# Attention and quantised network on one core: a longer lag for the network, a carried overshoot, GpSimd in the weights' quantisation, products of v in even pairs, an interleaved tail

## The chip, the cores and the metric

The kernel runs on one core of a Trainium2 chip. The core has five engines that work beside each other, each through its own instruction queue in order: TensorE (PE, matrix products), VectorE (DVE), ScalarE (ACT), GpSimd (POOL) and SyncE (SP), which here issues every DMA. The metric is the device time of one execution in microseconds; lower is better.

## The reference, cut to what matters

```python
xn = layernorm(x)                      # x: 8 x 1024 x 512, fp32
q, k, v = split(xn @ W_attn + b_attn)  # 16 heads of 32
att = softmax(causal(q @ k.T / sqrt(32)))
a = (att @ v) @ W_proj + b_proj
xq = fp4_quant_dequant(xn)             # blocks of 16 along the row
h = silu(xq @ wq_gate.T) * (xq @ wq_up.T)      # 1408 wide
f = fp4_quant_dequant(h) @ wq_down.T   # wq_*: weights quantised alike
out = x + a + f
```

Quantising a block takes its largest magnitude over 6 as a scale, divides, rounds to the values 0, 0.5, 1, 1.5, 2, 3, 4, 6 and multiplies by the scale again. Weights are quantised in the kernel too, 34 pieces of at most 128 x 512.

## The kernel before

The tokens are 64 tiles of 128 (8 batches of 8). Attention goes by 64 units: a unit is one pair of heads over one batch of 1024 tokens. All intermediate results between the stages lie in device memory: q and k in two halves each (high and low), v, the unnormalised y, the sums and their inverses, the transposed quantised tokens (xq_kept) and the network's result with the residual (part_kept).

Everything is written as Python generators, the streams. A stream issues some instructions and yields an estimated cost. `merge` always advances the stream that has used the smallest share of its total, so the order of the instructions on TensorE, ScalarE and SyncE is the order in which these generators were advanced. VectorE and GpSimd are ordered by the framework's scheduler. `Later(us, action)` puts an action (nearly always a DMA) off until so much estimated cost has passed.

The streams, with their lines:

- `begin` / `prepare` (L266): transposes a normalised tile (L215), keeps its quantised form, calls `load_tokens` for the tile after next and `normed` (L252, for later tiles with `quantised`, result xs) for the next tile. For each second tile it runs `project` (L307): q, k, v for 256 tokens (matmuls L315, L352), six chunks, weights from `ring_a`, two buffers of 512 KB.
- `quantised` (L182): ten VectorE instructions for a tile: L195 the block maximum, L196 to L198 small ones, L201 to L208 six of the full width.
- `weights_quantised` (L218): for each of the 34 pieces load, `quantised`, and one piece later the transposes on TensorE (L215) and ScalarE's copy (L216) into wgT, wuT or wdT.
- `prepare_late` (L282): the first eight tiles' tokens for the network, put off from the opening.
- `maxima` (L395): the row maxima of a unit's scores: matmuls L407, VectorE's mask L415 and reduce L417; at its end shT (L435).
- `weigh` (L438): scores again, with the maximum subtracted by a matmul (L466, L469), ScalarE's exponential (L477), GpSimd's causal zeroing of the diagonal block (L480), and the products with v (L449), which `weighted` issues for one or two key blocks j at a time. Two heads use different columns of the array, 33 columns each.
- `network` (L527): gate and up products (L557), `hidden`, the down products (L542); L539 adds the bias to the residual on GpSimd, L549 adds acc, and the sum part is stored. The jobs are issued in pairs.
- `finish` (L613): loads y and the inverses, multiplies (L625), multiplies by W_proj (L632, weights from `ring_p`, two loads of 512 KB a tile through one buffer), loads part and adds (L637), stores the output.

The opening interleaves `begin` of tiles 0 to 7 with EARLY = 11 pieces of weights, then does `begin` of tiles 8 and 9 beside the first unit's maxima. The main loop then runs over n = 0 to 63 and merges: `begin(n + 10)` while there are tiles (total 21.5 for odd n, 1.0 for even n), `finish` of tile n - 9 from n = 9 on, `weigh` of unit n, `maxima` of unit n + 1, and either, for n below LAG = 5, a fifth of the remaining weight pieces and of the late tiles, or, from n = 5 on, one tile's worth of the network through `up_to(net, TILE)`. After the loop five rounds run the rest of the network with the finishes, then the rest.

The lines that pick the groups of v's products:

```python
if j % 2 == 1 and waiting:
    yield weighted()
    waiting = []
waiting += fresh
```

Of the kernel before, what the change touches and what calls it, by code (L numbers as in the profile page):

```python
# [19 lines left out]
P = 128  # L20
# [7 lines left out]
def kernel(  # L28
# [44 lines left out]
    AHEAD = 10  # L73
    LAG = 5
    SCALE = HD**-0.5
# [11 lines left out]
    p8 = ctx.enter_context(tc.tile_pool(name="p8", bufs=8))  # L87
    dram = ctx.enter_context(tc.tile_pool(name="dram", bufs=3, space=DRAM))
    ps_g = ctx.enter_context(tc.tile_pool(name="ps_g", bufs=6, space=PSUM))
# [56 lines left out]
    class Ring:  # L146


        def __init__(self, pool, name, src):
            self.pool, self.name, self.src = pool, name, src  # L150
            self.cols = itertools.cycle(range(0, src.shape[2], 2 * P))
            self.loaded = []

        def load(self):
            col = next(self.cols)
# [6 lines left out]

    ring_a = Ring(p2, "wa", wa_in)
    ring_p = Ring(p1, "wp", wp_in)
# [16 lines left out]

    def quantised(src, w, xs):  # L182
# [18 lines left out]
        nc.vector.tensor_tensor(blocks(xs), blocks(src), spread(inv), ALU.mult)  # L201
        nc.vector.tensor_scalar(
            step.bitcast(I32), xs.bitcast(I32), 0x7F800000, None, ALU.bitwise_and
        )
        nc.vector.tensor_scalar(step, step, 1.0, 1.5 * 2.0**22, ALU.max, ALU.mult)
        nc.vector.tensor_tensor(xs, xs, step, ALU.add)
        nc.vector.tensor_tensor(xs, xs, step, ALU.subtract)
        nc.vector.tensor_tensor(blocks(xs), blocks(xs), spread(scale), ALU.mult)  # L208
        return xs
# [8 lines left out]
    def weights_quantised():  # L218
# [14 lines left out]
        for k, piece in enumerate(pieces):  # L233
            if k + 2 < len(pieces):
                loaded.append(load(*pieces[k + 2]))
            raw = loaded.pop(0)
            done.append((piece, quantised(raw, piece[4], raw)))
            yield 0.0
# [199 lines left out]
    def weigh(un):  # L438
        f, r0 = un.u * HU // HPC, un.u * HU % HPC
        for Q in range(2):  # L440
# [19 lines left out]
            for j in range(last + 1):  # L460
# [29 lines left out]
                yield (W - q0) * 0.00044 * 4  # L490
                if j % 2 == 1 and waiting:
                    yield weighted()
                    waiting = []
# [31 lines left out]


    def network(tiles):  # L527
        def turn(job):
# [4 lines left out]
        def down(job):  # L533
# [13 lines left out]
            if i == NI - 1:  # L547
                xr = tl.xr
                nc.vector.tensor_tensor(xr, tl.acc, xr, ALU.add)  # L549
                tl.part = dram.tile([P, D], F32, name="part_kept", bufs=NT + 6)  # L550
                Later(8.0, lambda: nc.sync.dma_start(out=tl.part, in_=xr))
            yield 0.1
# [21 lines left out]

        def load(tl):
            tl.xqT = p3.tile([P, NC, P], F32, name="xqT_in")
            nc.sync.dma_start(out=tl.xqT, in_=tl.xq)

        def jobs():
            load(tiles[0])  # L580
            for tl, following in zip(tiles, tiles[1:] + [None]):
# [7 lines left out]
        while True:  # L589
# [21 lines left out]
            older = pair  # L611

    def finish(tl):  # L613
        t = tl.t
        yT = p1.tile([P, NC, P], F32, name="yT")
        nc.sync.dma_start(out=yT, in_=tl.batch.y[:, :, t * P : (t + 1) * P].rearrange("f p t -> p f t"))
# [9 lines left out]
        yield 3.0  # L626
        po = ps_g.tile([P, D], F32, name="g")
        for half in range(2):
            cols = slice(half * 2 * P, (half + 1) * 2 * P)
            wp = ring_p.take()  # L630
            for c in range(NC):
                nc.tensor.matmul(po[:, cols], lhsT=yT[:, c, :], rhs=wp[:, c, :], start=(c == 0), stop=(c == NC - 1))  # L632
            ring_p.load()
            yield 1.7
        part = p3.tile([P, D], F32, name="res")
        nc.sync.dma_start(out=part, in_=tl.part)
        nc.vector.tensor_tensor(part, po, part, ALU.add)  # L637
        Later(6.0, lambda: nc.sync.dma_start(out=out[tl.b, t * P : (t + 1) * P, :], in_=part))
# [14 lines left out]
    class Tile:  # L653
        def __init__(self, n):
            self.n, self.b, self.t = n, n // NT, n % NT

    class Unit:
# [4 lines left out]
    def run(step):  # L662
        for cost in step:
            passed(cost)
# [12 lines left out]

    def up_to(step, total):

        spent = 0.0  # L680
        while spent < total:
            try:
                cost = next(step)
            except StopIteration:
                return
            spent += cost
            yield cost

    N = B * NT
# [11 lines left out]
    with tc.manual_schedule(  # L701
# [10 lines left out]
        PIECES = sum((w.shape[0] // P) * -(-w.shape[1] // CW) for w in (w_gate, w_up, w_down))  # L712
        EARLY = PIECES // 3
        weights_steps = weights_quantised()
        head = itertools.chain(*[begin(n) for n in range(NT)])
        merge([(head, 10.7 * NT), (up_to(weights_steps, EARLY * 0.5), EARLY * 0.5)])
        for un in units:
# [14 lines left out]
        merge([(itertools.chain(begin(NT), begin(NT + 1)), 22.0), (first_maxima(), 8.0)])  # L732
        load_biases()
        for n in range(N):
            streams = []
            if n + 2 < N:
# [11 lines left out]
            if n + AHEAD < N:  # L748
                streams.append((begin(n + AHEAD), 21.5 if n % QT == QT - 1 else 1.0))
            if n >= NT + 1:  # L750
                streams.append((finish(tiles[n - NT - 1]), 6.4))
            streams.append((weigh(units[n]), 19.0))
            if n >= LAG:
                streams.append((up_to(net, TILE), TILE))
            else:
                part = (PIECES - EARLY) / LAG * 0.5
                streams.append((up_to(weights_steps, part + 0.01), part))
                for tl in tiles[n * NT // LAG : (n + 1) * NT // LAG]:
# [52 lines left out]
```

## Time and profile before

| | us |
|---|---|
| median of three runs (lowest, highest) | 4766.83 (4761.64, 4768.15) |
| the profiled execution, its run | 4757.63 |
| its span | 4755.9 |
| mean granted TensorE clock | 0.976 of full |

The profile comes from one execution. The span is the time from the first to the last recorded instruction of that execution; the run has some 2 us around it. Sums made from the trace are to be set against the span; the median of the other runs is 11 us above it.

To read it: the page gives each engine's busy time, then the span in 40 slices of 119 us with the busy share in tenths. A group's row has line, engine, operation, output and inputs, shapes, the count, the busy time and the mean of one in ns, then the engine's idle time just before and what ended it. The record counts an fp32 product as two TensorE instructions, since it makes two passes (1408 records for 704 products at L542); the products of L407, L466 and L469, in a reduced format, have one. Matmul ends are modelled, so distances from start to start are the better measure: 429 ns for a record of 512 columns in fp32, 216 ns for 256, 231 ns for 512 in the reduced format.

Times of units, from the stamps of L498 (the copy of y, last in a unit): units 0 to 4 end 50.7 to 65.2 us apart, later even and odd units alternate around 59 and 82 us, and from unit 54 on, without `begin`, they are some 58 us apart.

### The profile page before, as it was taken

The page shows a single profiled execution, that of the slowest core. Times are in us where ns is not written, and L with a number is a line of the kernel's source. Part 1 is how long each engine was busy: PE and PEld are TensorE (multiplying, and loading weights), DVE is VectorE, ACT ScalarE, POOL GpSimd, SP SyncE. Part 2 cuts the span into 40 slices and gives each one's busy share as a digit, 9 for nine tenths or more (in the row PEclk, how much of TensorE's full clock was granted, in tenths as well). Part 3 has the DMA queues.
Part 4 walks back from the last instruction along what each step waited for, and adds up shares of the span by engine and source line. Part 5 has one row for each costly group of instructions (what it writes and reads, how often), then busy time and mean ns, then how long its engine had stood idle before and what let it go on. Part 6 is the DMA issues. An engine that isn't in the chain of part 4 may idle for free.

```text
span 4755.9 us, 54933 instructions
## 1 busy us (share of the span) xinstructions
PE 4490.6 (94%) x17876; PEld 2693.5 (57%) x17876; DVE 2794.9 (59%) x6841; ACT 1505.3 (32%) x2906; POOL 491.1 (10%) x1177
## 2 busy tenths in 40 slices
PE   7677899999999999999999999999999999999995
PEld 6445555555555555655555656556556555555553
DVE  6698466655556565656655656555656654566542
ACT  2133333333333333333333333333333333333310
POOL 0011111110110110110110011010111110111100
PEclk9888999999999999999999999999999999999997
DMA  6644434444453453544454454443454444333233
GB/s 208 181 138 137 111 102 109 132 128 130 114 150 106 123 135 107 139 132 117 125 146 118 121 146 118 123 128 115 128 145 122 132 123 127 98 98 94 65 91 108
DMA packets 582590, 590.38 MB, mean 124 GB/s; under 512 B 131616, under 2 KB 445984, under 8 KB 582304
## 3 DMA queue, kind: packets, MB, share of 16 engines
q1 hardware_dynamic: 582304, 586.88, 44.7%
q8 instruction: 142, 2.33, 0.2%
q14 instruction: 144, 1.18, 0.1%
HBM read 434.12 MB, written 152.57 MB: 123 GB/s over the span
## 4 chain that ended last, share of the span: by engine, by line
PE 83%; DVE 7%; DMA 6%; issue 1%; ACT 1%; SPq 1%; POOL 0%; DVEq 0%; ACTq 0%; POOLq 0%
PE g L557 24%; PE acc L542 11%; PE y L449 10%; PE g L315 8%; PE g L407 6%; PE g L466 5%; PE g L469 5%; PE g L632 5%; PE g L352 4%; PE g L215 2%; DMA inv_y<-inv_kept 2%; DVE scale L195 1%; DMA wp<-in_L_attn_W_proj_dram 1%; DMA qs<-qk_kept 1%; PE g L433 1%
## 5 line engine op out<-in xcount | busy, mean ns | idle before, releaser
L477 ACT ACTIVATE pr<-g 128x512 f32<-128x512 f32 (+3 forms) x1536 | 668.7, 492 | 1082.0 <-PE g L469 1072.8
L417 DVE TENSOR_REDUCE neg<-g 128x1 f32<-128x512 f32 (+3 forms) x1024 | 585.3, 582 | 230.0 <-PE g L407 225.7
L466 PE MATMUL g<-shT,pick 128*128 128x512 f32 (+3 forms) x1536 | 672.2, 447 | 20.3 <-DVE neg L417 16.3
L557 PE MATMUL g<-wgT,xqT_in 128*128 128x512 f32 (+1 forms) x1536 | 674.9, 566 | 13.8 <-DMA xqT_in<-xq_kept 13.4
L407 PE MATMUL g<-ks,qs 128*128 128x512 f32 (+3 forms) x1536 | 664.0, 477 | 18.5 <-DVE neg L417 11.4
L542 PE MATMUL acc<-wdT,hqT 128*128 128x512 f32 x1408 | 672.2, 599 | 1.4 <-ACT hqT L216 1.4
L480 POOL TENSOR_SCALAR_AFFINE_SELECT pr<-pr 128x128 f32<-128x128 f32 x1024 | 360.0, 366 | 3021.8 <-ACT pr L477 3005.5
L557 PE MATMUL g<-wuT,xqT_in 128*128 128x512 f32 (+1 forms) x1536 | 671.5, 562 | 0.0
L449 PE MATMUL y<-pr,vs 128*33 128x512 f32 (+3 forms) x3072 | 606.8, 497 | 2.9 <-POOL pr L480 2.7
L415 DVE TENSOR_TENSOR g<-g,mask 128x128 f32<-128x128 f32 x1024 | 289.3, 293 | 482.4 <-PE g L407 477.1
L469 PE MATMUL g<-qs,ks 128*128 128x512 f32 (+3 forms) x1536 | 516.9, 348 | 0.0
L315 PE MATMUL g<-xnT,wa 128*128 128x256 f32 x2048 | 486.9, 393 | 29.4 <-DVE scale L196 12.9
L315 PEld LDWEIGHTS g<-xnT,wa 128*128 128x128 f32 x2048 | 398.4, 198 | 108.2 <-ACT xnT L216 13.9
L407 PEld LDWEIGHTS g<-ks,qs 128*128 128x128 f32 x1536 | 280.4, 191 | 306.1 <-issue 139.8
L557 PEld LDWEIGHTS g<-wgT,xqT_in 128*128 128x128 f32 x1536 | 278.5, 191 | 237.5 <-issue 184.1
L557 PEld LDWEIGHTS g<-wuT,xqT_in 128*128 128x128 f32 x1536 | 276.0, 189 | 216.4 <-issue 167.8
L542 PEld LDWEIGHTS acc<-wdT,hqT 128*128 128x128 f32 x1408 | 255.7, 189 | 230.4 <-issue 215.0
L466 PEld LDWEIGHTS g<-shT,pick 128*128 128x128 f32 x1536 | 293.6, 191 | 154.4 <-issue 65.7
L469 PEld LDWEIGHTS g<-qs,ks 128*128 128x128 f32 x1536 | 293.8, 191 | 96.8 <-issue 64.6
L449 PEld LDWEIGHTS y<-pr,vs 128*33 128x33 f32 x3072 | 138.9, 110 | 354.5 <-issue 278.2
L572 DVE TENSOR_TENSOR hid<-hid,g 128x512 f32<-128x512 f32 (+1 forms) x192 | 122.7, 639 | 306.8 <-PE g L557 288.7
L632 PE MATMUL g<-wp,yT 128*128 128x256 f32 x1024 | 253.3, 392 | 47.5 <-DVE yT L625 27.9
(87 smaller groups left out, 4201.2 us busy)
## 6 DMA issues: line engine op xcount, KB each, us to landing
wa<-in_L_attn_W_attn_dram SPq DMA_DIRECT2D x194, 512.0 KB
wp<-in_L_attn_W_proj_dram SPq DMA_DIRECT2D x131, 512.0 KB
qs<-qk_kept SPq DMA_DIRECT2D x512, 128.0 KB
ks<-qk_kept SPq DMA_DIRECT2D x512, 128.0 KB
qk_kept<-high SPq DMA_DIRECT2D x128, 256.0 KB
qk_kept<-low SPq DMA_DIRECT2D x128, 256.0 KB
res<-in_L_attn_x_dram SPq DMA_DIRECT2D x72, 256.0 KB
v_kept<-v SPq DMA_DIRECT2D x64, 264.0 KB
```

Source lines behind the costliest of these rows:

```text
L315: nc.tensor.matmul(pq[:, j, :], lhsT=wa[:, c, j * P : (j + 1) * P], rhs=xnT[:, c, :], start=(c == 0), stop=(c == NC - 1),)
L407: nc.tensor.matmul(sc[:, :n], lhsT=un.qs[Q][:, r, i * P : (i + 1) * P], rhs=un.ks[h][:, r, :n], start=True, stop=True,)
L415: nc.vector.tensor_tensor(sc[:, n - P : n], sc[:, n - P : n], mask, ALU.add)
L417: nc.vector.tensor_reduce(dst, sc[:, :n], AX.X, ALU.max, negate=True)
L449: nc.tensor.matmul(y[r * 2 * HD : r * 2 * HD + VW, q0:], lhsT=un.vs[h][:, jj, r, :], rhs=pr[:, q0:], start=(j == 0), stop=(j == last), ski ...
L466: nc.tensor.matmul(w[:, q0:], lhsT=pick[:, Q * HU + r, :], rhs=un.shT[:, q0:], start=True, stop=False)
L469: nc.tensor.matmul(w[:, q0:], lhsT=un.ks[h][:, r, jj * P : (jj + 1) * P], rhs=un.qs[Q][:, r, q0:], start=False, stop=True,)
L477: nc.scalar.activation(pr[:, q0:], w[:, q0:], AF.Exp)
L480: nc.gpsimd.affine_select(out=pr[:, q0 : q0 + P], in_=pr[:, q0 : q0 + P], compare_op=ALU.is_ge, fill=0.0, base=0, pattern=[[1, P]], channe ...
L542: nc.tensor.matmul(tl.acc, lhsT=job.hqT[:, j, :], rhs=wdT[:, i, :], start=(i == 0), stop=(i == NI - 1))
L557: nc.tensor.matmul(job.g[:, : job.w], lhsT=job.tl.xqT[:, c, :], rhs=wT[:, c, job.i0 : job.i0 + job.w], start=(c == 0), stop=(c == NC - 1),)
L632: nc.tensor.matmul(po[:, cols], lhsT=yT[:, c, :], rhs=wp[:, c, :], start=(c == 0), stop=(c == NC - 1))
```

## The change

Eight edits go together:

- LAG is 8 instead of 5, and EARLY is half of the 34 pieces (17) instead of a third (11). So 17 pieces and eight late tiles are spread over eight units.
- `quantised` takes an engine for its first and last full-width product; the weights pass GpSimd.
- `weighted` is called at even j instead of odd j.
- `up_to` carries what it spent too much (or too little) into its next call.
- `begin(n + 10)` of even n has a total of 4.0 instead of 1.0.
- `finish` of tile n - 10 instead of n - 9; it loads part ahead of the products where it is there already, with its store done first if that is still put off, and makes the product in two halves with a PSUM tile and an addition each.
- From unit 55 on, W_proj stays resident in the two buffers of `ring_a`, whose loads are counted so that none comes too many.
- After the loop each of eight rounds takes one tile of the network and one finish (two in the first); the last finish begins its loads before the rest of the network.

```diff
-    LAG = 5
+    LAG = 8
...
-            done.append((piece, quantised(raw, piece[4], raw)))
+            done.append((piece, quantised(raw, piece[4], raw, nc.gpsimd)))
...
-        nc.vector.tensor_tensor(blocks(xs), blocks(src), spread(inv), ALU.mult)
+        spreader = spreader or nc.vector
+        spreader.tensor_tensor(blocks(xs), blocks(src), spread(inv), ALU.mult)
...
-        nc.vector.tensor_tensor(blocks(xs), blocks(xs), spread(scale), ALU.mult)
+        spreader.tensor_tensor(blocks(xs), blocks(xs), spread(scale), ALU.mult)
...
-                if j % 2 == 1 and waiting:
+                if j % 2 == 0 and waiting:
...
-                tl.part = dram.tile([P, D], F32, name="part_kept", bufs=NT + 6)
-                Later(8.0, lambda: nc.sync.dma_start(out=tl.part, in_=xr))
+                tl.part = dram.tile([P, D], F32, name="part_kept", bufs=NT + 8)
+                tl.stored = Later(8.0, lambda: nc.sync.dma_start(out=tl.part, in_=xr))
...
+        def load_part():
+            tl.stored.now()
+            part = p3.tile([P, D], F32, name="res")
+            nc.sync.dma_start(out=part, in_=tl.part)
+            return part
...
-        po = ps_g.tile([P, D], F32, name="g")
+        part = load_part() if tl.part is not None else None
         for half in range(2):
+            po = ps_g.tile([P, 2 * P], F32, name="g")
             cols = slice(half * 2 * P, (half + 1) * 2 * P)
-            wp = ring_p.take()
+            wp = resident[half] if resident else ring_p.take()
             for c in range(NC):
-                nc.tensor.matmul(po[:, cols], lhsT=yT[:, c, :], rhs=wp[:, c, :], start=(c == 0), stop=(c == NC - 1))
-            ring_p.load()
+                nc.tensor.matmul(po, lhsT=yT[:, c, :], rhs=wp[:, c, :], start=(c == 0), stop=(c == NC - 1))
+            if not resident:
+                ring_p.load()
+            if part is None:
+                part = load_part()
+            nc.vector.tensor_tensor(part[:, cols], po, part[:, cols], ALU.add)
             yield 1.7
-        part = p3.tile([P, D], F32, name="res")
-        nc.sync.dma_start(out=part, in_=tl.part)
-        nc.vector.tensor_tensor(part, po, part, ALU.add)
...
-    def up_to(step, total):
-
+    def up_to(step, total, over=[0.0]):
+
+        total += over[0]
         spent = 0.0
         while spent < total:
...
             spent += cost
             yield cost
+        over[0] = total - spent
...
-        EARLY = PIECES // 3
+        EARLY = PIECES // 2
...
+            if n == N - AHEAD + 1:
+                for half in range(2):
+                    wp = p2.tile([P, NC, 2 * P], F32, name="wa")
+                    nc.sync.dma_start(out=wp, in_=wp_in[:, :, half * 2 * P : (half + 1) * 2 * P])
+                    resident.append(wp)
...
-                streams.append((begin(n + AHEAD), 21.5 if n % QT == QT - 1 else 1.0))
-            if n >= NT + 1:
-                streams.append((finish(tiles[n - NT - 1]), 6.4))
+                streams.append((begin(n + AHEAD), 21.5 if n % QT == QT - 1 else 4.0))
+            if n >= LAG + 2:
+                streams.append((finish(tiles[n - LAG - 2]), 6.4))
...
+                if n == LAG - 1:
+                    Later(20.0, lambda: load(tiles[0]))
...
-        left = [finish(tiles[n]) for n in range(N - NT - 1, N)]
-        for n in range(N - LAG, N):
-            count = 1 if n in (N - LAG, N - 1) else 2
-            some, left = left[:count], left[count:]
-            merge([(up_to(net, TILE), TILE), (itertools.chain(*some), 6.4 * count)])
-        next(left[0])
+        for n in range(N, N + LAG):
+            some = [finish(tiles[m]) for m in ([n - LAG - 2] if n == N else []) + [n - LAG - 1]]
+            merge([(up_to(net, TILE), TILE), (itertools.chain(*some), 6.4 * len(some))])
+        end = finish(tiles[N - 1])
+        passed(next(end))
         run(net)
-        for step in left:
-            run(step)
+        run(end)
```

More of the change, by code (lines that the diff above doesn't have):

```diff
@@ L87 @@
     p8 = ctx.enter_context(tc.tile_pool(name="p8", bufs=8))
-    dram = ctx.enter_context(tc.tile_pool(name="dram", bufs=3, space=DRAM))
+    dram = ctx.enter_context(tc.tile_pool(name="dram", bufs=4, space=DRAM))
     ps_g = ctx.enter_context(tc.tile_pool(name="ps_g", bufs=6, space=PSUM))
@@ L146, with __init__ @@
     class Ring:
-        def __init__(self, pool, name, src):
-            self.pool, self.name, self.src = pool, name, src
+        def __init__(self, pool, name, src, count=None):
+            self.pool, self.name, self.src, self.count = pool, name, src, count
             self.cols = itertools.cycle(range(0, src.shape[2], 2 * P))
@@ L154, in load @@
         def load(self):
+            if self.count is not None:
+                self.count -= 1
+                if self.count < 0:
+                    return
             col = next(self.cols)
@@ L161, in take @@
             return self.loaded.pop(0)
-    ring_a = Ring(p2, "wa", wa_in)
+    ring_a = Ring(p2, "wa", wa_in, B * NT // QT * 3 * D // (2 * P))
     ring_p = Ring(p1, "wp", wp_in)
@@ L179, in load_biases, with quantised @@
             ring_p.load()
-    def quantised(src, w, xs):
+    def quantised(src, w, xs, spreader=None):
         nb = w // BLOCK
@@ L524, in invert, with load @@
             Later(12.0, lambda: nc.sync.dma_start(out=over(un.batch.inverses[un.u]), in_=z))
+    def load(tl):
+        tl.xqT = p3.tile([P, NC, P], F32, name="xqT_in")
+        nc.sync.dma_start(out=tl.xqT, in_=tl.xq)
     def network(tiles):
@@ L573, in hidden @@
             job.hq = quantised(job.hid, job.w, job.hid)
-        def load(tl):
-            tl.xqT = p3.tile([P, NC, P], F32, name="xqT_in")
-            nc.sync.dma_start(out=tl.xqT, in_=tl.xq)
         def jobs():
-            load(tiles[0])
             for tl, following in zip(tiles, tiles[1:] + [None]):
@@ L611, in network @@
             older = pair
+    resident = []
     def finish(tl):
         t = tl.t
+        def load_part():
[3 more added lines that the diff above has]
+            return part
         yT = p1.tile([P, NC, P], F32, name="yT")
@@ L655, in __init__ @@
             self.n, self.b, self.t = n, n // NT, n % NT
+            self.part = None
     class Unit:
@@ L676, in merge @@
                 live.remove(s)
-    def up_to(step, total):
+    def up_to(step, total, over=[0.0]):
+        total += over[0]
         spent = 0.0
         while spent < total:
-            try:
-                cost = next(step)
-            except StopIteration:
+            cost = next(step, None)
+            if cost is None:
                 return
@@ L712 @@
         PIECES = sum((w.shape[0] // P) * -(-w.shape[1] // CW) for w in (w_gate, w_up, w_down))
-        EARLY = PIECES // 3
+        EARLY = PIECES // 2
         weights_steps = weights_quantised()
         head = itertools.chain(*[begin(n) for n in range(NT)])
-        merge([(head, 10.7 * NT), (up_to(weights_steps, EARLY * 0.5), EARLY * 0.5)])
+        merge([(head, 10.7 * NT), (up_to(weights_steps, EARLY * 0.5, [0.0]), EARLY * 0.5)])
         for un in units:
@@ L733 @@
         load_biases()
+        late = [0.01]
         for n in range(N):
+            if n == N - AHEAD + 1:
[3 more added lines that the diff above has]
+                    resident.append(wp)
             streams = []
@@ L756 @@
                 part = (PIECES - EARLY) / LAG * 0.5
-                streams.append((up_to(weights_steps, part + 0.01), part))
+                streams.append((up_to(weights_steps, part, late), part))
+                if n == LAG - 1:
+                    Later(20.0, lambda: load(tiles[0]))
                 for tl in tiles[n * NT // LAG : (n + 1) * NT // LAG]:
```

## The prediction

> **What bounds the kernel now.** I read the page's engine and slice lines first, to see who is the bound and where it isn't.
>
> ```profile
> PE 4490.6 (94%) x17876; PEld 2693.5 (57%) x17876; DVE 2794.9 (59%) x6841; ACT 1505.3 (32%) x2906; POOL 491.1 (10%) x1177
> PE   7677899999999999999999999999999999999995
> PEclk9888999999999999999999999999999999999997
> ```
>
> TensorE is the bound from the fifth slice to the last but one. The first 500 us and the last 60 us are where it is not, and there its clock is lower too. So I cut the span at the stage borders, which I took from the stamps of L435 (one per attention unit) and of L498 (end of a unit): the opening, units 0 to 4 (no network in them), units 5 to 63, the tail. The windows view gives, for each: length, then busy us of PE, PEld, DVE, ACT, POOL, then clock, DMA share, GB/s.
>
> ```profile
> 13.00:144.00 131.00, 109.58 (x489) 91.38 (x488) 84.17 (x190) 28.50 (x61) 4.88 (x8) 0.93 0.71 223
> 144.00:194.00 50.00, 28.25 (x109) 21.71 (x107) 32.37 (x87) 5.61 (x12) 0.55 (x1) 0.83 0.70 194
> 194.00:489.00 295.00, 218.51 (x1000) 143.21 (x1000) 249.35 (x655) 95.81 (x206) 42.86 (x94) 0.84 0.46 128
> 489.00:4557.00 4068.00, 3990.78 (x15866) 2356.03 (x15865) 2358.85 (x5763) 1361.54 (x2605) 433.95 (x1052) 0.99 0.44 121
> 4557.00:4756.00 199.00, 143.12 (x418) 80.72 (x416) 65.32 (x133) 12.53 (x22) 4.03 (x3) 0.87 0.35 105
> ```
>
> In units 0 to 4 VectorE is busy 85% and TensorE waits for it; POOL is nearly free. The waits view, first in 194:489, then in 600:4500, and the rows of the costliest groups say what stands behind it:
>
> ```profile
> PE g L215 <- DVE hid L208: 48.4, 3, 17.4
> PE g L466 <- DVE neg L417: 13.0, 7, 4.7
> ...
> PE g L215 <- DVE xs L208: 39.6, 11, 7.8
> ...
> DVE res L637 <- DMA res<-part_kept: 218.8, 26, 23.3
> ...
> L539 POOL TENSOR_TENSOR res<-res,bp 128x512 f32<-128x512 f32 x64 | 85.0, 1328 | 597.4 <-DMA res<-in_L_attn_x_dram 467.4 <-DVE hid L207 37.6 <-DVE hid L572 33.8
> ```
>
> Three stalls of up to 17 us for a quantised weight piece early; eleven stalls later for xs, the quantised tokens of the next tile; and VectorE standing at L637 for the reload of part. The chain's last lines show the tail: each of the last finishes is serial.
>
> ```profile
> 4710.64 4.29 DMA inv_y<-inv_kept
> 4714.95 0.05 DVEq L625
> 4715.15 0.70 DVE yT L625
> 4715.89 3.79 PE g L632 x8
> 4719.70 3.83 DMA wp<-in_L_attn_W_proj_dram
> 4723.57 3.42 PE g L632 x8
> ```
>
> One finish costs 21 us there (4715.9 to 4736.8), of which 7 us are products at a falling clock; elsewhere its 16 products take 3.45 us.
>
> **What the Trainium skill says.** "TensorEngine Tiling (Array Packing)", Key Properties: changing the tiling mode drains TensorE. The trace agrees: L449 is 33 columns wide, and a group of its products takes 0.34 us (one j) or 0.37 us (two j) more than start-to-start times of the same shapes give, against 0.06 us for a stretch without one. "GPSIMD Engine Reference", 3.1: an elementwise tensor_tensor costs 1.96 times VectorE's. Here L539 has 1328 ns, VectorE's like shapes 690 ns: 1.92. "Advanced Engine Details and Errata", VectorE Performance Modes: the second SBUF port is shared and the two interfere. Ten two-input VectorE instructions that lie beside an L539 average 0.97 us, the others 0.69 us. "TensorE: Matmul & The Clock Gate", What's actually happening: half clock after an idle window of 3.4 us. The trace has 143 us at half clock before 505 us and about 40 between there and 4600.
>
> **The change, part by part**, against the profiled execution's span (4755.9 us; its run 4757.6, the median of the runs 4766.8, so I add 11 at the end).
>
> *v's products in even pairs.* Before, a unit's groups are j0, j1-2, j3 for the first half and j0, 1-2, 3-4, 5-6, 7 for the second: 8. After: 2 and 4. Two groups fewer in each of 64 units, 128 x 0.30 us (0.35 less the 0.06 background) = 38 us, all on TensorE. Bounds: 30 and 45. In every unit that is 0.6 us. The products of j are still issued one j behind their exponentials, so no new wait.
>
> *Opening (0 to 194).* EARLY goes from 11 to 17 pieces. A piece on VectorE is 4.8 us (reduce 0.68, small ones 0.70, four of 0.69, two of 0.43); with the first and last product on GpSimd 3.5 us. So 17 x 3.5 - 11 x 4.8 = +7 us of VectorE, plus its wait at L207 for GpSimd: 1.33 us and some issue, at most 17 x 1.5 = 25 us, plus slower neighbours (0.28 us each). TensorE gets 6 x 0.44 us of transposes. VectorE is 64% busy in 13:144, so most is covered by its gaps; what is not delays xt, at whose transposes TensorE already stops 3 to 5 us, four times. I take +15; bounds 0 and +45. The rstd power on GpSimd now queues behind the products; that is in it.
>
> *Units without network: 8 instead of 5.* Before 295 us, 59 a unit. VectorE per unit after: maxima and small ones 18.5 (1121 us of L415 and L417 over 64 units, plus 1), begin 8.9, one late tile 6.6, 17/8 pieces of 3.5 = 7.5: 41.5 in single durations. Before, the same sum is 5 x 27.4 + 22 x 4.8 + 8 x 6.6 = 295, of which the overlapping of neighbours leaves 249 busy, in 295 us elapsed. So what 41.5 takes is about 41.5 us, and 3 to 4 for GpSimd waits: 45. TensorE per unit: scores, maxima and v 21.3, groups 1.8, begin 11.2, transposes 1.4: 36, but 26 in even units and 46 in odd ones (project falls in those). Even: VectorE's 40; odd: TensorE's 46 at a clock of 0.92: 50. Again 45. The stage is 8 x 45.5 = 365 (bounds 304: TensorE's 36 at 0.95; 472: 59 as now). The affine_selects now share GpSimd's queue with 4.3 products of 1.33 a unit, 6 us of 45; that cover holds unless VectorE is late for GpSimd. load(tiles[0]) before unit 8 removes the 13.4 us wait of L557 for xqT_in at 489.
>
> *Units with network: 56 instead of 59.* From L498: units 13 to 52 take 71.3 us each, units 55 to 62 (no begin) 58.4. Off these: 0.6 for the groups; 0.45 for the carried overshoot (before, 59.9 network tiles lay in 59 units, 0.9 x 29.5 us; this moves work into the tail and is no gain); and in units with begin 1.4 for stalls: 50 us of TensorE gaps over 1 us between 600 and 4500, of which 40 wait for xs, and some 16 lost at half clock, over 49 units. They go because begin at 4.0 instead of 1.0 puts the next tile's normed and quantised at a quarter of an even unit, not at its end where L637 stands in the way too; part is now asked for at half a unit and before wp, not behind it. What is late next there: nothing over 1 us that I find. 46 x 68.9 + 10 x 57.4 - 7 (no finish in two units) = 3736. The same sum for before gives 4077 against 4068 measured, so I take 3727. Bounds: 3700 and 3800 (the stalls stay, 66 us).
>
> *Tail.* Before, 199 us for 4.1 tiles and 9 finishes. After: 8 tiles at 30.5 (33.3, 38.3, 37.1 us between ends of acc, less 3.45 for each finish beside them) = 244, nine finishes 31, 3 for hidden waits. wp stays in two buffers that the attention ring has left, so no 3.6 us load between halves; yT and inv of the last tile are loaded ahead. Then acc's add 0.7, store 4.5, reload 4.6 (4.1 landing at the end of before), add 0.7, store 3.0: 14. Together 292. Bounds 285 and 320.
>
> Queues: the moved part load is one DMA a finish, issued by SP ahead of two wp loads instead of behind them; the 131 wp loads fall by 38 (the last 19 finishes use the kept copies). dram's fourth buffer, part_kept's two and the Ring's count cost nothing: they allocate, or stop two loads nobody takes.
>
> Sum: 194 + 15 + 365 + 3727 + 292 = 4593, 163 below 4755.9. On the median: 4766.8 - 163 = 4604.
>
> **Rivals.** (1) *The early units stay at VectorE's pace, 59 us*, since it stands still while GpSimd works: 8 x 59 = 472, 4711. For: VectorE's order is strict, and L207 comes directly behind its GpSimd producer. Against: a wait of 1.5 us cannot eat what 1.3 us less per piece and the thinner spread (2.1 pieces a unit, not 4.6) give. (2) *They fall to TensorE's pace*: 304, 4543. For: VectorE reached 85% before. Against: odd and even units differ by 20 us of TensorE work. (3) *The change doesn't do what it says in the long stage*: pairs save little since merge cuts the stream anew and the xs stalls only move: +38 +60, 4702. For: the drain is paid at each switch, whoever follows. Against: groups are counted in the order of issue, 6 a unit. (4) *Slower*: GpSimd's in-order queue, with affine_selects and rstd in it, holds each piece, and VectorE behind it, in the opening and the early units. At 10 us instead of 1.5 a piece it is 17 x 8.5 = 145 in units and some 115 in the opening: 4864. It decides from 7 us a piece. For: POOL waits in order. Against: POOL is 15% busy in 194:489.
>
> **How the numbers follow.** Forecast 0.50, (1) 0.15, (2) 0.14, (3) 0.13, (4) 0.08. The likeliest is 4604. Its own bounds, taken as independent, give about 4555 to 4660; taking in most of (1), (2) and (3) the range is 4530 to 4712. Faster by over 0.2% (9.5 us, about what a measurement can tell here): the first four, 0.91; slower 0.08; within, 0.01.
>
> **What would show it.** 384 groups of L449 instead of 512; unit stamps 45 us apart in units 0 to 7, and 1.5 to 2 us closer in pairs later; no L215 wait for xs; GpSimd products of 1.3 to 1.5 us; PEclk near 0.9 in the early units; one finish after the last acc, some 14 us. I am wrong if GpSimd's broadcast product takes over 3 us, if early units stand above 55, or if the tail's tiles lie above 35 us.

## The result and the profile after

The changed kernel takes 4774.91 us (median of 14 runs), the kernel before 4765.12 us (14 runs beside them): ratio 1.0024, 95% interval 1.0016 to 1.0032. It is slower by some 10 us where 163 us less were forecast. The profiled execution has a span of 4773.9 us.

The page's engine and slice lines of the changed kernel:

```profile
PE 4510.9 (94%) x17876; PEld 2724.1 (57%) x17876; DVE 2764.2 (58%) x6837; ACT 1483.7 (31%) x2892; POOL 548.3 (11%) x1245
PE   7678899999999999999999999999999999999999
PEclk9789999999999999999999999999999999999999
```

The tail is now full to the end, as planned. TensorE's busy time has grown by 20 us with the same 17876 records: "busy" counts modelled ends, so the sum of the work can't be read from it. The windows view, cut at the same borders (opening in two parts, early units, units with the network, tail; columns as before):

```profile
13.00:164.00 151.00, 115.19 (x505) 96.15 (x504) 97.42 (x215) 31.03 (x67) 42.22 (x42) 0.87 0.65 202
164.00:213.00 49.00, 29.56 (x115) 22.96 (x114) 31.57 (x84) 5.51 (x12) 3.71 (x4) 0.81 0.76 203
213.00:616.00 403.00, 331.86 (x1564) 223.13 (x1565) 284.56 (x762) 143.64 (x315) 85.72 (x176) 0.92 0.52 143
616.00:4493.00 3877.00, 3762.75 (x14888) 2237.06 (x14887) 2198.82 (x5458) 1273.73 (x2449) 401.04 (x996) 0.99 0.43 117
4493.00:4774.00 281.00, 270.98 (x808) 144.19 (x806) 146.80 (x303) 28.55 (x51) 10.25 (x8) 1.00 0.19 59
```

| stage | before | forecast | after |
|---|---|---|---|
| opening | 194 | 209 | 213 |
| early units (5; 8; 8) | 295 | 365 | 403 |
| units with the network (59; 56; 56) | 4068 | 3727 | 3877 |
| tail (network tiles: 4.1; 8; 8) | 199 | 292 | 281 |

So 150 us of the miss lie in the long stage and 38 in the early units; the tail is better than forecast by 11. In the long stage a pair of units with `begin` (an even and an odd one, from the stamps of the copy of y, units 14 to 53) takes 143.8 us on average. Forecast were 2 x 68.85 = 137.7, before had 142.5. The waits view of TensorE for the long stage (700 to 4400 us), then for the early units (us in total, times, longest):

```profile
PE g L412 <- DVE neg L422: 41.1, 22, 1.9
PE g L471 <- ACT hid L578: 24.1, 22, 1.1
PE g L471 <- ACT pr L482: 16.7, 22, 1.0
...
PE y L454 <- POOL pr L485: 21.8, 16, 6.1
PE g L438 <- DVE scale L200: 14.8, 3, 5.2
PE g L220 <- POOL hid L213: 12.5, 2, 9.7
```

The stalls for xs are gone, as forecast. In their place are waits that are there 22 times, once for each pair of units in the window: 41 us in sum for a place in PSUM, where the products land, that VectorE's maxima (L422) hold, and smaller ones. Before, the same wait stood there 4 times (600 to 4500 us):

```profile
PE g L407 <- DVE neg L417: 5.5, 4, 2.5
```

The pairs are alike to a fraction of a us: the fastest takes 143.0 us, the middle one 143.6. A stall that is in one is in all.

What VectorE does then, from the timeline of one pair (start, duration, instruction; lines between left out):

```profile
1488.69 0.62 DVE L422 TENSOR_REDUCE neg<-g 128x1 f32<-128x512 f32 x1
...
1489.43 0.69 DVE L206 TENSOR_TENSOR hid<-hid,inv 128x512 f32<-128x512 f32 x1
1490.04 0.68 DVE L206 TENSOR_TENSOR xs<-xt,inv 128x512 f32<-128x512 f32 x1
...
1494.39 0.68 DVE L213 TENSOR_TENSOR hid<-hid,scale 128x512 f32<-128x512 f32 x1
1494.99 0.68 DVE L213 TENSOR_TENSOR xs<-xs,scale 128x512 f32<-128x512 f32 x1
1495.60 0.29 DVE L420 TENSOR_TENSOR g<-g,mask 128x128 f32<-128x128 f32 x1
1495.80 0.68 DVE L422 TENSOR_REDUCE neg<-g 128x1 f32<-128x512 f32 x1
```

and TensorE's side of it (the bracket is the idle time before, and what ended it):

```profile
1493.91 0.50 PE L471 MATMUL g<-shT,pick 128*128 128x512 f32 x1 [0.75 <-ACT pr L482]
1494.26 0.40 PE L474 MATMUL g<-qs,ks 128*128 128x512 f32 x1
1496.53 0.58 PE L412 MATMUL g<-ks,qs 128*128 128x256 f32 x1 [1.88 <-DVE neg L422]
```

Two quantisations, the network's hid and the next tile's xs, run interleaved from 1489 to 1495.6, and between a maximum's end and the next mask lie 6.3 us. TensorE goes on as long as it has places in PSUM, stops for 1.9 us, and goes on at half clock for 3.4 us. In 700 to 4400 us the trace's clock record has 75 us at half clock, before the change 38.

The chain's last lines show the tail: the last down products, the addition of acc, the store and the reload of part (lines between left out).

```profile
4761.26 2.86 PE acc L551 x6
...
4764.19 0.70 DVE res L558
...
4764.91 2.02 DMA part_kept<-res
...
4766.95 2.92 DMA res<-part_kept
```

### The profile page after: what moved, and what is told of

The parts are those of the page before. It is cut to its first block, busy times and chain, and to the rows that moved or that the text cites. A ratio compares the mean times of both kernels' runs of the same rounds, so it can differ in the third digit from the quotient of the medians.

```text
span 4773.9 us, 55008 instructions
## 1 busy us (share of the span) xinstructions
PE 4510.9 (94%) x17876; PEld 2724.1 (57%) x17876; DVE 2764.2 (58%) x6837; ACT 1483.7 (31%) x2892; POOL 548.3 (11%) x1245
## 4 chain that ended last, share of the span: by engine, by line
PE 79%; DVE 8%; ACT 3%; DMA 2%; issue 2%; POOL 1%; SPq 0%; ACTq 0%; DVEq 0%; POOLq 0%
PE g L566 23%; PE acc L551 12%; PE y L454 10%; PE g L320 8%; PE g L412 5%; PE g L471 5%; PE g L646 5%; PE g L474 4%; PE g L357 4%; PE g L220 2%; DVE neg L422 1%; ACT pr L482 1%; DMA qs<-qk_kept 1%; DVE scale L199 1%; DMA inv_y<-inv_kept 1%
## 5 line engine op out<-in xcount | busy, mean ns | idle before, releaser
L412 PE MATMUL g<-ks,qs 128*128 128x512 f32 (+3 forms) x1536 | 725.3, 509 | 66.4 <-DVE neg L422 44.7
L551 PE MATMUL acc<-wdT,hqT 128*128 128x512 f32 x1408 | 695.3, 617 | 1.4 <-ACT hqT L221 1.4
L485 POOL TENSOR_SCALAR_AFFINE_SELECT pr<-pr 128x128 f32<-128x128 f32 x1024 | 346.3, 350 | 2661.1 <-ACT pr L482 2649.5
L471 PE MATMUL g<-shT,pick 128*128 128x512 f32 (+3 forms) x1536 | 599.5, 398 | 55.2 <-ACT hid L578 24.1
L422 DVE TENSOR_REDUCE neg<-g 128x1 f32<-128x512 f32 (+3 forms) x1024 | 583.0, 580 | 102.4 <-PE g L412 94.8
L412 PEld LDWEIGHTS g<-ks,qs 128*128 128x128 f32 x1536 | 285.4, 193 | 327.2 <-issue 147.9
L551 PEld LDWEIGHTS acc<-wdT,hqT 128*128 128x128 f32 x1408 | 266.6, 197 | 259.2 <-issue 235.3
L454 PEld LDWEIGHTS y<-pr,vs 128*33 128x33 f32 x3072 | 159.7, 110 | 406.3 <-issue 235.9
L471 PEld LDWEIGHTS g<-shT,pick 128*128 128x128 f32 x1536 | 294.6, 192 | 163.7 <-issue 45.3
L331 ACT ACTIVATE full<-g,bqk 128x256 f32<-128x256 f32 x256 | 107.4, 471 | 625.8 <-PE g L412 265.0
L638 DVE TENSOR_TENSOR yT<-yT,inv_y 128x512 f32<-128x512 f32 x64 | 44.1, 689 | 431.6 <-DMA inv_y<-inv_kept 363.5
```

Source lines behind the costliest of these rows:

```text
L412: nc.tensor.matmul(sc[:, :n], lhsT=un.qs[Q][:, r, i * P : (i + 1) * P], rhs=un.ks[h][:, r, :n], start=True, stop=True,)
L422: nc.vector.tensor_reduce(dst, sc[:, :n], AX.X, ALU.max, negate=True)
L454: nc.tensor.matmul(y[r * 2 * HD : r * 2 * HD + VW, q0:], lhsT=un.vs[h][:, jj, r, :], rhs=pr[:, q0:], start=(j == 0), stop=(j == last), ski ...
L471: nc.tensor.matmul(w[:, q0:], lhsT=pick[:, Q * HU + r, :], rhs=un.shT[:, q0:], start=True, stop=False)
L485: nc.gpsimd.affine_select(out=pr[:, q0 : q0 + P], in_=pr[:, q0 : q0 + P], compare_op=ALU.is_ge, fill=0.0, base=0, pattern=[[1, P]], channe ...
L551: nc.tensor.matmul(tl.acc, lhsT=job.hqT[:, j, :], rhs=wdT[:, i, :], start=(i == 0), stop=(i == NI - 1))
```

## The experiments

All edits are to the changed kernel unless said otherwise. "Pair" is the mean of pairs of units 14 to 53 in the profile, "early" the time of one early unit. Three of the eight edits were not undone alone: `finish` in halves, the resident W_proj and the interleaved tail.

| run | us | ratio to before (95% interval) | pair | early |
|---|---|---|---|---|
| before | 4765 | 1 | 142.5 | 59.3 |
| changed | 4774.9 | 1.0024 (1.0016, 1.0032) | 143.8 | 50.4 |
| e1_begin_late | 4880.1 | 1.0241 (1.0228, 1.0255) | 148.3 | 50.9 |
| e2_odd_pairs | 4690.9 | 0.9845 (0.9832, 0.9859) | 139.8 | 52.1 |
| e3_lag5 | 4732.2 | 0.9935 (0.9923, 0.9948) | 141.3 | 56.7 |
| e4_dve_only | 4765.4 | 0.9998 (0.9990, 1.0006) | 144.0 | 50.0 |
| e5_no_carry | 4748.9 | 0.9968 (0.9955, 0.9980) | 143.2 | 50.5 |
| e6_pause | 4722.3 | 0.9911 (0.9899, 0.9924) | 141.6 | 50.5 |
| e7_late_own_tile | 4778.5 | 1.0025 (1.0016, 1.0034) | 144.0 | 51.2 |
| e8_odd_begin_late | 4815.6 | 1.0108 (1.0095, 1.0122) | 145.7 | 51.0 |
| e9_odd_lag5 | 4737.7 | 0.9943 (0.9930, 0.9955) | 142.2 | 56.6 |
| e10_before_begin4 | 4719.5 | 0.9910 (0.9895, 0.9925) | 140.6 | 57.8 |
| e11_odd_no_carry | 4684.2 | 0.9829 (0.9815, 0.9842) | 140.2 | 52.1 |
| e12_odd_lag5_dve | 4728.5 | 0.9926 (0.9913, 0.9938) | 142.2 | 57.4 |
| e13_begin2 | 4700.3 | 0.9862 (0.9848, 0.9875) | 139.9 | 51.2 |
| e14_odd_begin2 | 4652.4 | 0.9761 (0.9748, 0.9775) | 137.7 | 52.4 |
| e15_all_early | 4797.7 | 1.0067 (1.0053, 1.0080) | 144.0 | 46.9 |
| e16_pause_begin2_free | 4664.1 | 0.9786 (0.9772, 0.9799) | 139.7 | 51.1 |
| e17_pause_begin2 | 4673.2 | 0.9808 (0.9793, 0.9823) | 139.4 | 51.0 |
| e18_odd_begin2_dve | 4635.6 | 0.9729 (0.9714, 0.9744) | 137.5 | 51.5 |

### One edit undone at a time

The place of begin:

```diff
-                streams.append((begin(n + AHEAD), 21.5 if n % QT == QT - 1 else 4.0))
+                streams.append((begin(n + AHEAD), 21.5 if n % QT == QT - 1 else 1.0))
```

> The changed kernel with one number undone: begin of even units has the total 1.0 again instead of 4.0. Theory A (bunching): at 4.0 each even unit does its transposes, copies and the next tile's quantisation in its first quarter, beside the network's quantisation and, early, beside a late tile that needs the same xqT buffer. Then each pair of units loses some 4.5 us of TensorE in the long stage and each even unit of the first eight some 10 us. Expected 4774.9 - 23 x 4.5 - 4 x 10 = about 4630, less what xs stalls come back (at most 50): 4630 to 4680, and the first eight units at 45 us each. Theory B (the gain went elsewhere: drains, the carried overshoot, the lag): within 20 us of the changed kernel. Theory C: the xs stalls come back in full, above 4775.

It was 105 us slower than the changed kernel: theory C. The waits of TensorE in its long stage:

```profile
PE g L220 <- DVE xs L213: 133.7, 22, 6.9
PE g L471 <- ACT hid L578: 24.0, 22, 1.1
```

The stall for xs, which before had in 11 places, is there in each pair, 6 us long. So the new place is worth a lot here, and bunching at 4.0 is not the whole answer; but what this run compares with is a stall that is worse than before's.

The grouping:

```diff
-                if j % 2 == 0 and waiting:
+                if j % 2 == 1 and waiting:
```

> The changed kernel with v's products in the old grouping (8 groups a unit instead of 6). If the pairs gave what I counted, 128 more groups of 0.30 us: 38 us slower than the changed kernel, about 4813. If the wait for the last exponentials and their causal zeroing ate the gain (theory B): within 10 us of it.

84 us faster than the changed kernel, where 38 us slower or no difference was expected. The new grouping, priced with the narrowest bounds of all, costs 84 us here. I count a group from the start of the record before it to the start of the second record after it, less what records of the same shapes take from start to start elsewhere. By this count a pair of units (14 to 53) spends 6.6 us on six groups a unit and 6.5 us on eight: nothing was saved. The last group of each half is why: with six groups it takes 0.42 to 1.18 us, 0.70 on average, with eight 0.34. Nothing of its own stream lies between the scores of the last block j and the products that need its exponentials and their zeroing.

The 4.0 us by which the pairs differ lie in the order of the other streams. TensorE's waits in the long stage are, with the old grouping,

```profile
PE g L471 <- DVE neg L422: 19.0, 27, 2.2
PE g L412 <- ACT pr L482: 17.6, 26, 0.7
PE g L471 <- ACT pr L482: 16.4, 22, 0.7
```

With one more of 0.7 us these are 54 us in sum, where the changed kernel's are 108, and L412's stall for the maxima is not there. At half clock TensorE spends 7 us instead of 75. In both kernels the two quantisations run interleaved in each of the 20 even units from 14 to 53. But here the next maximum or mask comes after 4.9 us instead of 6.3, and TensorE stands for 0.7 us at L412 instead of 1.9.

The lag (with two finishes in each of five last rounds):

```diff
-    LAG = 8
+    LAG = 5
...
-            if n >= LAG + 2:
-                streams.append((finish(tiles[n - LAG - 2]), 6.4))
+            if n >= 10:
+                streams.append((finish(tiles[n - 10]), 6.4))
```

> The changed kernel with LAG 5: weights and late tiles spread over five units, network from unit 5 on, finish still of tile n - 10, two finishes in each of five last rounds. If stages without the network cost what they do in the changed kernel (50 us a unit against 36 of TensorE work), three such units fewer and three tiles more beside attention give 3 x 14 = 42 us less, minus what five units pay for more weight pieces each: 4735 to 4760. If the lag is neutral: within 10 us of the changed kernel. If the lag was a gain: above 4785.

43 us faster than the changed kernel, just below the range named. Taken alone this reads as a loss by the longer lag. The later run with the old grouping corrects it. With LAG 5 the two quantisations meet in none of the 20 even units.

GpSimd's share:

```diff
-            done.append((piece, quantised(raw, piece[4], raw, nc.gpsimd)))
+            done.append((piece, quantised(raw, piece[4], raw)))
```

> The changed kernel with the weights' quantisation on VectorE alone. By my sum GpSimd saves 17 x 1.3 = 22 us of VectorE in the first eight units and costs about 10 in the opening: 10 to 25 us slower than the changed kernel. If GpSimd's queue is what holds the early units (rival 4 in small), it is 20 us or more faster.

10 us faster without GpSimd, neither of the two. The opening takes 202 us instead of 213, the early units 400 instead of 403. The products on GpSimd were not slow (in the changed kernel 1.17 and 1.10 us for 128x512), but VectorE's time saved in the early units bought nothing, and in the opening GpSimd's share cost 11 us.

### What the lock and the wait are worth

The lock: with the carried overshoot each pair of units repeats the one before, so a stall in one is in all. The wait: that of the last groups for their exponentials.

The network's overshoot not carried (the same in the tail's rounds):

```diff
-                streams.append((up_to(net, TILE), TILE))
+                streams.append((up_to(net, TILE, [0.0]), TILE))
...
```

> The changed kernel without the carried overshoot for the network (each unit's call starts from zero; the weights keep theirs). With the carry the traces repeat from pair to pair to a tenth of a us, so a stall that falls in one pair falls in all 20. Theory P (phase lock): without it stalls come in some pairs only, and each unit with the network takes 0.45 us of it ahead: 20 to 60 us faster than the changed kernel, 4715 to 4755. Theory Q: stalls are set by what lies in a quarter unit, not by the lock: within 12 us.

26 us faster, as theory P said. Its pairs range from 138.7 to 153.3 us, where the changed kernel's lie between 143.0 and 146.0. The mean of the pairs is nearly the same (143.2). The units with the network take the same in sum, 14 us less with `begin` and 13 more without, and the tail 257 us instead of 281, since each unit took a little of the network ahead. So the pairs are locked by the carry, but nearly all that this run gains is work taken out of the tail at no cost elsewhere, not stalls, which theory P had in mind.

A pause ahead of the last groups:

```diff
+            yield 1.5
             yield weighted()
             yu = p2.tile([P, W], F32, name="yu")
...
-            streams.append((weigh(units[n]), 19.0))
+            streams.append((weigh(units[n]), 22.0))
```

> The changed kernel with an idle entry of cost 1.5 in the stream ahead of the last group of v's products of each half (and 22 instead of 19 for the stream's total), so that other streams' work lies between the last scores and the products that need their exponentials. Theory W (the last group waits for the last exponentials and their zeroing, on TensorE): the wait of some 2.1 us a pair of units in the long stage goes, groups stay at six with 0.33 us each: 50 us or more faster than the changed kernel, below 4725. Theory Q (the new grouping only moves the other streams): no clear gain, within 20 us of 4775.

53 us faster, as theory W said. By the count above the groups take 5.2 us a pair of units instead of 6.6, the last ones 0.46 us on average instead of 0.70. The weight loads' wait for GpSimd's zeroing in the long stage, first of the changed kernel, then of this one:

```profile
PEld y L454 <- POOL pr L485: 88.2, 201, 0.8
```

```profile
PEld y L454 <- POOL pr L485: 24.3, 43, 0.8
```

The pause moves the other streams too, so not all of the 53 us is this wait. The quantisations still run interleaved in all 20 even units, but L412's stall for the maxima is gone, and at half clock TensorE spends 48 us instead of 75. Shorter waits stand in its place, about as much in sum:

```profile
PE g L471 <- DVE neg L422: 24.5, 42, 1.7
PE g L412 <- ACT pr L482: 23.7, 48, 0.7
```

A late tile's tokens put back into their own tile:

```diff
-        xqT = p1.tile([P, NC, P], F32, name="xqT")
+        if own:
+            xqT = xq.rearrange("p (c e) -> p c e", e=P)
+        else:
+            xqT = p1.tile([P, NC, P], F32, name="xqT")
...
```

> The changed kernel in which a late tile's transposed tokens go back into the tile they came from, so that it doesn't share the one xqT buffer with the tile of begin. ScalarE stood 9.7 us for that buffer's store in an even early unit, and v's products waited 6 us behind it. If that is what made the first eight units 403 us instead of the 365 forecast: 20 to 35 us faster than the changed kernel, 4740 to 4755, with the early even units some 6 us shorter. If VectorE's load is what sets them: within 8 us.

No gain. ScalarE's wait for the buffer's store (44 us in the early units) is gone, but the early units take as long with other waits in its place (the lines of this kernel are three further down):

```profile
PE g L415 <- ACT full L334: 22.2, 4, 6.0
PE g L220 <- DVE res L213: 21.0, 3, 7.4
PE g L220 <- POOL hid L213: 13.7, 2, 9.8
```

Old grouping and old place of begin (the edits of the first two runs together):

> The changed kernel with both undone: old grouping of v's products and begin of even units at 1.0. At 1.0 with the new grouping the stall for xs was there in each pair of units (6 us). If that is the stall's own doing, this is about 105 us slower than with the old grouping and 4.0 (4691): 4780 to 4810. If grouping and place of begin act on each other, it lies below 4750.

4816, so 125 us slower than with the old grouping and 4.0, a little above the range named: TensorE waits 22 times for xs, 124 us in sum. With the carry that stall comes whatever the grouping.

### Two edits at once, and one alone

Old grouping and LAG 5:

> The changed kernel with the old grouping of v's products and LAG 5. If the two losses are independent: 4775 - 84 - 43 = about 4648. If LAG 5 gained only because it shifted the streams against the new grouping: 4680 to 4700.

Neither: 4738, 47 us slower than the old grouping with LAG 8. So the lag's sign depends on the grouping: 43 us lost by LAG 8 with the new one, 47 gained with the old one. The grouping's sign depends on the lag as well: at LAG 5 the new one is 6 us the faster (4732 against 4738). The pairs say why it cannot be priced alone: 141.3 (5, new), 143.8 (8, new), 142.2 (5, old), 139.8 (8, old). With LAG 5 and the old grouping a stall of 2.5 us for VectorE's shift (L438) comes in each pair.

The kernel before with begin of even units at 4.0, nothing else:

```diff
-                streams.append((begin(n + AHEAD), 21.5 if n % QT == QT - 1 else 1.0))
+                streams.append((begin(n + AHEAD), 21.5 if n % QT == QT - 1 else 4.0))
```

> The kernel before with one number of the change alone: begin of even units at 4.0. If the place of begin removes the xs stalls by itself (40 us of waits and some 15 of half clock in the trace of before): 4700 to 4720. If it needs the carry, since only with it the stall falls in every pair: 4740 to 4765.

4719.5, 46 us faster than before, as its first theory said: no stall for xs is among the waits listed for its long stage, whose smallest is 1.7 us in sum.

Old grouping, no carry:

> The changed kernel with the old grouping and without the carried overshoot. With the new grouping taking the carry away gave 26 us. Theory P (the lock repeats whatever stall there is): with the old grouping there is less to repeat, so it gives less than 10 us, 4680 to 4700. Theory R (the carry costs by itself, through work that comes later): 20 us or more faster than 4691.

7 us faster than with the carry: P again.

Old grouping, LAG 5, VectorE alone:

> As the run with the old grouping and LAG 5, with the weights' quantisation on VectorE alone. At LAG 8 that was 10 us faster, all of it in the opening. With 3.4 pieces a unit instead of 2.1 VectorE has more to do in the five early units: between 10 us faster and 15 us slower than that run.

9 us faster than with GpSimd, 13 of it in the opening, 4 lost in the early units.

### The collision

```diff
-                streams.append((begin(n + AHEAD), 21.5 if n % QT == QT - 1 else 4.0))
+                streams.append((begin(n + AHEAD), 21.5 if n % QT == QT - 1 else 2.0))
```

> The changed kernel with a total of 2.0 for begin of even units: the next tile's normalisation and quantisation come at half the unit instead of a quarter. Theory K (collision with the network's quantisation in the first quarter): the stall of 2 us and the half clock after it go, 3 us or more a pair, 4700 to 4730. Theory M (each place collides with something, since the order is the same in every pair): within 20 us of 4775.

4700, 75 us faster than the changed kernel: theory K. The pairs fall by 3.9 us, and the waits in the long stage are

```profile
PE g L471 <- ACT hid L578: 24.0, 22, 1.1
PE g L412 <- ACT full L331: 10.9, 23, 0.5
PE y L454 <- POOL pr L485: 8.1, 27, 0.6
...
PE g L412 <- DVE neg L422: 6.1, 22, 0.3
```

L412's wait for VectorE has gone from 41 to 6 us, that of L471 for pr is gone; ACT's 24 us stand as before. At half clock TensorE spends 3 us instead of 75, and the two quantisations meet in none of the 20 even units.

The same with the old grouping:

> The same with the old grouping. Theory K: its stall at that place is smaller (0.9 us), so it gains less: 4660 to 4685 against 4691. Theory M: between 4680 and 4740.

4652, better than both theories said. Its pairs take 137.7 us, which is what the prediction had for the changed kernel.

All 34 pieces in the opening:

```diff
-        EARLY = PIECES // 2
+        EARLY = PIECES
...
```

> The changed kernel with all 34 weight pieces in the opening. If VectorE's and GpSimd's load with pieces is what holds the early units, they fall from 50.4 us to 42 to 44 each; if the order of the streams is, they stay above 48. The opening grows by 17 pieces of 3.5 to 5 us: 270 to 300 us instead of 213. In sum 4775 to 4815 in the first case, 4820 to 4850 in the second.

Between the two: the early units fall to 46.9 us, the opening grows to 255 us. By the working of the prediction an early unit without pieces would take 42 us (34 by VectorE in even ones, 50 by TensorE in odd ones), so the pieces' load explains 3.5 us a unit, and some 5 us are left that no load explains.

Pause, begin at 2.0, no carry:

> The changed kernel with the pause ahead of the last groups, begin of even units at 2.0, and no carry for the network. If the wait, the collision and the lock are what the new grouping loses, pairs now give their 1.2 us a pair of units over the old grouping: 4640 to 4675, below all others. If the streams' new order brings a stall of its own wherever it falls: 4690 to 4730.

4664, within the first range, but not below the old grouping with begin at 2.0. To tell the carry from the grouping, the same with the carry:

> New grouping with the pause ahead of its last groups, begin of even units at 2.0, carry kept. If six groups are worth their 1.2 us a pair of units and nothing else differs: 4610 to 4635, 30 us below the old grouping's 4652. If the grouping pays in how it lets the other streams through: 4645 to 4690.

4673, 21 us above the old grouping's 4652: the second theory. Against the changed kernel with 2.0 alone (4700) the pause gives 27 us. Its groups take 4.9 us a pair of units, 6.5 with the old grouping, and its pairs are still 1.7 us longer. Waits of L471 for hid (1.1 us in each pair) and for maxima show where part of this lies; the rest was not settled.

The best version found, old grouping, begin at 2.0, VectorE alone:

> The old grouping, begin of even units at 2.0, and the weights' quantisation on VectorE alone. With the changed kernel that gave 9.5 us and at LAG 5 9 us, nearly all in the opening: 4635 to 4650 here. If GpSimd's share helps once the early units stall less: above 4655.

4635.6 us, 2.7% below the kernel before (ratio 0.9729, 0.9714 to 0.9744), 139 us below the changed kernel. Its page:

```profile
PE 4461.2 (96%) x17876; PEld 2686.2 (58%) x17876; DVE 2803.4 (61%) x6905; ACT 1477.4 (32%) x2892; POOL 463.9 (10%) x1177
PE   7678899999999999999999999999999999999999
```

## Why the prediction was wrong

**The step that failed first: "v's products in even pairs".** It read "The products of j are still issued one j behind their exponentials, so no new wait", and took 38 us of gain with bounds of 30 and 45. That is true of all groups but the last of each half. In the old grouping the last group held one j, and the group before it was issued between it and the last scores. In the new one it holds two j, right behind the last scores, and the two heads' products, which should run side by side, stand for the exponential and the zeroing of the very last block. The drains saved (four a pair of units, 1.2 us) came back as that wait: 6.6 against 6.5 us a pair, so none of the 38 us came. The pause shows the wait: with other work in between, the groups fall to 5.2 us a pair. In time that was worth 53 us at 4.0, where the pause also changed the stall of the next step, and 27 us at 2.0, where that stall is small.

In the changed kernel the grouping costs 84 us in all, so the term was off by 122 us, most of the miss of 173. No bound of mine held a loss. The 84 us are hardly the groups' own time. They lie in waits elsewhere, L412's stall and the half clock after it first of all. So the two failed steps overlap, and their shares can't be added up: the grouping costs 84 us with `begin` at 4.0 and 48 at 2.0, where that stall is small but waits remain that the old grouping lacks (L471 for hid, 24 us); at LAG 5 it gains 6.

**"What is late next there: nothing over 1 us that I find."** This was the second. The prediction moved the next tile's quantisation to a quarter of the even unit and did not ask what VectorE has to do there. In the changed kernel it is where the network's quantisation falls: 6.3 us without a maximum, and TensorE stops for 1.9 us in every pair. The place alone doesn't set the size: with 4.0 and the old grouping the two run interleaved as well, but TensorE stops for 0.7 us, and with 4.0 and LAG 5 they don't meet. Moving the same work to the middle of the unit gave 75 us with the new grouping, and 39 with the old one. Both steps are one mistake: an edit was priced by its own instructions, in an order that is made anew by merge for every edit. None of the three signs of being wrong that the prediction named came (the early units lie below 55 us on average). What failed was its line on the pairs, which should end 1.5 to 2 us closer and ended 1.3 us further apart.

**Stalls for xs.** Right: they went, and in the kernel before the new place alone gave 46 us; the sum had 1.4 us for 46 units, 64 us. There the size was off. VectorE's standing for the reload of part, 219 us before, fell to 2 us, but in the same stage it stood 406 us for the inverses (L638) instead of 59. Whether that held up maxima, no run tests.

**Early units.** 50.4 us instead of 45.5, 38 us in sum. VectorE is busy 71% there, not at its limit as my sum had it, and relief helps little: without GpSimd's share they take 50.0, without the shared buffer 51.2, without any piece in them 46.9. What sets the rest may be the order in which the engines wait for each other; no run here isolates it, so it stays open.

**GpSimd.** The cost in the opening was about right (+15 forecast for GpSimd and two other causes, +19 measured, of which 11 go away with VectorE alone), the saving in the early units (22 us of VectorE) turned out to be worth nothing.

**Opening, tail.** 209 and 292 forecast, 213 and 281 measured. The tail's tiles and the resident weights came as worked out; store and reload of part were shorter (2.0 and 2.9 us from issue to landing, where I had 4.5 and 4.6; the last reload of before took 4.1).

**The overshoot.** It was priced as work moved and no gain or loss. With the new grouping it is a loss: the units with the network take the same with and without the carry, and the tail is 24 us longer with it. With the old grouping the run without it is 7 us faster. The carry also makes all pairs alike, which the prediction did not see: with it a stall is in none or in each of some 22 pairs. The spread of the pairs without it, 138.7 to 153.3 us, shows it.

**Rivals.** Rival (3), that pairs save little and stalls only move, had the mechanism and put it at 4702 with a chance of 0.13. It did not go far enough: there is no reason why an edit's stalls, once moved, should be no larger than they were. Rival (1) had the early units at 59 us, they came a third of the way. The slower rival through GpSimd's queue did not occur: VectorE waited 9.6 us in all for L206 in the early units.

## What to carry to other kernels

Where the order of an in-order engine is made by interleaving streams, an edit's price is its own instructions plus a new order for all others, and the second part can be larger and of either sign: the lag alone was worth -43 or +47 us, depending on the grouping. Forecast such an edit by walking through one period of the new order, engine by engine, and by asking for each moved piece what lies beside it on the engine that it needs. Ahead of the last use in a loop put work of another stream, since the last group has no next iteration to hide its wait; here that gave 53 and 27 us, though the old grouping stayed the faster one.

## What the runs showed that I had not expected

- A drain saved is no time saved if the group that remains has to wait: two heads' products that run side by side (7 ns apart in the trace) ran one after the other when the second head's exponential and zeroing were late: from the first to the last start of a block of 128 columns up to 0.49 us instead of 0.14.
- Equal periods amplify: 22 stalls of 1.9 us in 22 pairs, and after most of them 3.4 us or more at half clock. A gap of 1.9 us, with one of 0.75 us shortly before it, is less than the idle window of 3.4 us that the prediction cites; what is measured decides.
- A stall removed by a buffer (9.7 us of ScalarE standing for the store of xqT) came back elsewhere: early units of 51.2 instead of 50.4 us.
